# Layer 0's attention: where the softmax sums of a batch are turned into divisors

## The chip, the cores and the metric

The kernel runs on one core of a Trainium2 chip. The metric is the device time of one execution in microseconds (us). Before the change it was 2256.95 us, the median of three runs (2251.18 to 2261.61). A core has engines with queues of their own: TensorE (PE; its weight loads are shown as PEld), VectorE (DVE), ScalarE (ACT), GpSimd (POOL), and SyncE (SP), which here only sends DMAs. Each engine takes its instructions in the order in which they were laid down and waits at an instruction until what it needs is there.

## The reference, cut to what matters

The reference is a four-layer decoder on x of 4 batches, 512 tokens and 128 channels; each layer adds an attention, a cross-attention and a feed-forward part of experts to x. The change touches layer 0's attention alone: 16 heads of 8 channels, causal, with a bias that falls with distance.

```python
att = jnp.einsum('bqhd,bkhd->bhqk', q, k) * scale
att = att / temperature
bias = slopes[:, None, None] * rel[None, :, :]
bias = jnp.where(causal[None, :, :], bias, -jnp.inf)
w = jax.nn.softmax(att + bias[None], axis=-1)
y = jnp.einsum('bhqk,bkhd->bqhd', w, v).reshape(Bc, Tc, Cc)
return y @ W_proj + b_proj
```

So for each batch, query and head there is a sum of exponentials by which 8 channels of y are divided before the projection. x receives the projected y.

## The kernel before, in words

`l0_attn` goes over 16 items, each a batch b and a group g of four heads, in rounds. In round r four items are in work at once: the scores and maxima of item r (`score_units`, eleven units of one or more heads), the exponentials of item r-1 (`exp_units`, ten units; the first five early, at the end of the round, the others late, in the next), the values of item r-2 (`values`), and, where item r-3 closes a batch, the division and the projection of that batch. A round has steps i = 0 to 10. Round 6 is that of batch 0's division, round 10 that of batch 1, round 14 that of batch 2.

The steps in a round that matter here:

- `shift` (i = 0) splits the negated maxima of the item before into three bf16 parts on VectorE; `shift_rows` (i = 2) transposes them on TensorE (L1165), copies them on ACT (`d_rows`, L1167) and puts them into the stacked queries `qs` with four DMAs (L1169). The exponentials of that item read them, first the early ones.
- `load` (i = 7) fetches the stacked parts of queries and keys of item r+2 with six DMAs (L1125, L1126).
- `project`, in the second round of a batch, makes queries and keys of the next batch, splits them into bf16 parts `q3` and `k5`, and sends these to DRAM with four DMAs (`q_parts`, `k_parts`, L1109 and L1111).
- `values` multiplies exponentials by values. The value tile has 32 columns a head, of which 8 are channels and the ninth is one, so the ninth row of a head in the result is its sum of exponentials. ACT copies the result into `ys[b]` (L1207): 128 partitions (four heads of 32 rows), four groups, 512 tokens.
- `sums` (i = 9, in the round in which the last group's values are made) brings the sums into rows of tokens: 16 products of y with a selecting matrix give 128 x 4 x 16; VectorE inverts them (L1219) and splits them into three bf16 parts (`in_three`, from L1290).
- `divide` (i = 1 of the next round) transposes these parts (`turned3`, L1301), copies them on ACT (L1303), spreads each group's inverses over the heads' rows with a product by `pick`, and multiplies y by that, four times 128x512 (L436 is the helper of all such operations, L425 that of all dense products).
- `close` (i = 4 of that round) projects y with 16 products and adds the result to x.

Beside the rounds another chain is woven in at a fixed rate of steps: the norms of the other batches, the small products of the context, then layer 0's cross-attention of batches 0 and 1 and the router of the first two batches (`route`, whose small steps on VectorE end in `w_halves` on POOL, eight transposes on TensorE at L665 and `w_turned`). The order written in the program is not the final one: a planner with its own costs lays the instructions of each engine in an order, in which an instruction may pass others of its engine that are not ready by its reckoning.

Of the kernel before, what the change touches and what calls it, by code (L numbers as in the profile page):

```python
# [13 lines left out]
F32 = mybir.dt.float32  # L14
BF16 = mybir.dt.bfloat16
# [3 lines left out]
ALU = mybir.AluOpType  # L19
# [3 lines left out]
P = 128  # L23
B, S, D = 4, 512, 128
# [267 lines left out]
class Net:  # L292
# [745 lines left out]
    def l0_attn(self, pool, W, Wo):  # L1038
# [3 lines left out]
        nc, tc = self.nc, self.tc  # L1042
# [30 lines left out]
        def biases():  # L1073
            ps = self.mm((1, D))
            self.dot(ps, *[(Wo["bv"][:, g : g + 1], Wo["wp"][:, g * D : g * D + D]) for g in range(4)])
            br = one([1, D], "br")
            self.tt(br, ps, Wo["bp"], ALU.add)
            wp0 = one([P, D], "wp0")
            nc.vector.tensor_copy(wp0, Wo["wp"][:, :D])
            nc.sync.dma_start(wp0[8:9, :], br)  # L1080
            wp.extend([wp0] + [Wo["wp"][:, g * D : g * D + D] for g in range(1, 4)])

        items = [(b, g) for b in range(B) for g in range(4)]
        made, ys, stacks = {}, {}, {}

        def project(b):

            xb = self.tokens(b)
            pq, pk = self.mm(), self.mm()
            self.dot(pq, (W["wq"], xb))  # L1090
            self.dot(pk, (W["wk"], xb))
            q, k = (pool.tile([P, S], F32, tag=n, name=n, bufs=1) for n in "qk")
            nc.vector.tensor_scalar(q, pq, W["bq"], sc, ALU.add, ALU.mult)
            nc.scalar.activation(k, pk, AF.Identity, bias=W["bk"])
            yield
            q3, k5 = pool.tile([P, 3, S], BF16, tag="q3", name="q3"), pool.tile([P, 5, S], BF16, tag="k5", name="k5")
            for a, out in ((q, q3), (k, k5)):
                nc.scalar.copy(out[:, 0], a)
                self.tt(a, a, out[:, 0], ALU.subtract)
            yield  # L1100
            for a, out in ((q, q3), (k, k5)):
                nc.scalar.copy(out[:, 1], a)
                self.tt(out[:, 2], a, out[:, 1], ALU.subtract)
            yield
            nc.gpsimd.tensor_copy(k5[:, 3:5], k5[:, 0:2])
            qd = self.away.tile([16, 24, S], BF16, name=f"q_parts{b}")
            kd = [self.away.tile([16, 24, S], BF16, name=f"k_parts{b}_{c}") for c in range(3)]
            flat = lambda d: d.rearrange("h (d p) t -> (h d) (p t)", p=3)
            nc.sync.dma_start(flat(qd), q3.rearrange("r p t -> r (p t)"))  # L1109
            for c in range(3):  # L1110
                nc.sync.dma_start(flat(kd[c]), k5[:, c : c + 3].rearrange("r p t -> r (p t)"))  # L1111
            stacks[b] = qd, kd
            yield
            ps = self.mm((P, TB, 16, 8))
            for j in range(TB):
                self.dot(ps[:, j].rearrange("p h d -> p (h d)"), (self.tile_of(TB * b + j), W["wv"]))
            nc.scalar.copy(vs[b % 2][:, :, :, :8], ps)
            yield

        def load(b, g):  # L1120

            qd, kd = stacks[b]
            for c in range(3):
                r = slice(24 * c, 24 * c + 24)
                nc.sync.dma_start(qs[g][r], qd[4 * g : 4 * g + 4].rearrange("h r t -> r h t"))  # L1125
                nc.sync.dma_start(ks[g][r], kd[c][4 * g : 4 * g + 4].rearrange("h r t -> r h t"))  # L1126

        def score_units(b, g):

            m = made[b, g, "m"] = pool.tile([P, TB, 4], F32, tag="m", name="m", bufs=2)  # L1130

            def unit(i, h0, per):
                n = (i + 1) * P
                ps = self.mm((P, per, n))
                for h in range(per):
                    nc.tensor.matmul(  # L1136
                        ps[:, h], lhsT=qs[g][:K1, h0 + h, i * P : n], rhs=ks[g][:K1, h0 + h, :n], start=h == 0, stop=False
                    )
                nc.tensor.matmul(  # L1139
                    ps[:, :, i * P :], lhsT=self.identb, rhs=self.causal.unsqueeze(1).to_broadcast([P, per, P]),  # L1140
                    start=False, stop=True,
                )
                nc.vector.tensor_reduce(m[:, i, h0 : h0 + per], ps, AX.X, ALU.max, negate=True)  # L1143

            return [
                lambda i=i, h0=h0, per=per: unit(i, h0, per)
                for i, per in ((3, 1), (2, 1), (1, 2), (0, 4)) for h0 in range(0, 4, per)
            ]

        def shift(b, g):  # L1150

            m = made.pop((b, g, "m"))
            d3 = made[b, g, "d"] = pool.tile([P, TB, 4, 3], BF16, tag="d3", name="d3")
            rest = pool.tile([P, TB, 4], F32, tag="d_rest", name="d_rest")
            nc.vector.tensor_copy(d3[..., 0], m)
            self.tt(rest, m, d3[..., 0], ALU.subtract)
            nc.vector.tensor_copy(d3[..., 1], rest)
            self.tt(d3[..., 2], rest, d3[..., 1], ALU.subtract)
# [49 lines left out]

        inv = {}

        def sums(b):

            y = ys[b]
            ps = self.mm((P, TB, 4, 4))
            for j in range(TB):
                for g in range(4):
                    self.dot(ps[:, j, g], (y[:, g, j * P : j * P + P], W["sums"]))
            den = pool.tile([P, TB, 16], F32, tag="den", name="den")
            nc.vector.reciprocal(den, ps.rearrange("p j g h -> p j (g h)"))  # L1219
            inv[b] = pool.tile([P, TB, 3, 16], BF16, tag="s3", name="s3")  # L1220
            self.in_three(inv[b], den, pool, "s_rest")

        def divide(b):
            y = ys[b]
            dT = self.turned3(inv.pop(b), pool)
            for g in range(4):
                c = self.mm()
                self.dot(c, (pick[:, 4 * g : 4 * g + 4].rearrange("r h i -> r (h i)"), dT))
                self.tt(y[:, g, :], y[:, g, :], c, ALU.mult)

        def close(b):
            y = ys.pop(b)
            ps = self.mm((P, TB, D))
            for j in range(TB):
                self.dot(ps[:, j, :], *[(y[:, g, j * P : j * P + P], wp[g]) for g in range(4)])
            self.add_rows(b, ps)

        def rounds(first, last):
            n = len(items)
            item = lambda i: items[i] if 0 <= i < n else None  # L1240
            if first == 0:
                yield from project(0)
                load(0, 0)
                biases()
                load(0, 1)
                yield
            for r in range(first, last):
                now, prev, old, done = (item(r - i) for i in range(4))
                a = score_units(*now) if now else []
                if prev:  # L1250
                    made["units", prev] = exp_units(*prev)
                late = made.pop(("units", old))[5:] if old else []
                early = made["units", prev][:5] if prev else []
                ahead = project(now[0] + 1) if now and now[1] == 1 and now[0] + 1 < B else iter(())
                for i in range(11):
                    if i == 0 and prev:
                        shift(*prev)
                    if i == 2 and prev:
                        shift_rows(*prev)
                    if i < len(a):  # L1260
                        a[i]()
                    e = late[i : i + 1] if i < 6 else early[i - 6 : i - 5]
                    for unit in e:
                        unit()
                    yield
                    if i == 1 and done and done[1] == 3:
                        divide(done[0])
                        yield
                    if i == 4 and done and done[1] == 3:
                        close(done[0])  # L1270
                        yield
                    if i == 7 and old:
                        values(*old)
                        yield
                    if i == 9 and old and old[1] == 3:
                        sums(old[0])
                        yield
                    if i in (1, 3, 5, 8, 10):
                        next(ahead, None)
                    if i == 7 and item(r + 2):  # L1280
                        load(*item(r + 2))
# [1103 lines left out]
```

## Time and profile before

| what | us |
|---|---|
| median of three runs | 2256.95 |
| the profiled execution | 2272.79 |
| its span, first to last instruction | 2271.0 |
| TensorE busy in the span | 2109.5 (93%) |
| VectorE busy in the span | 1608.1 (71%) |
| layer 0's attention, in the span | about 20 to 280 |
| 16 products of the sums, batch 0 | 94.6 to 98.3 |
| 16 products of the projection, batch 0 | 106.5 to 110.1 |

A busy share is an average over stages with different limits. In the stage of the attention the engines follow one another closely, so the reader should look at the order of instructions in the stretch of a batch's division, at what each waits for, and at the TensorE clock that was granted there: it is a share of full speed, and the products of a stretch with 0.50 take twice their time. Times in the timeline are from the start of the span.

### The profile page before, as it was taken

What the parts mean: (1) busy time and instruction counts of PE and PEld (TensorE: products, weight loads), DVE (VectorE), ACT (ScalarE), POOL (GpSimd) and SP (SyncE); (2) the same over time, 40 slices, a digit from 0 to 9 for tenths busy, and PEclk for the clock granted to TensorE, in tenths of its full rate; (3) what the DMA queues carried; (4) which work ended last, traced back from release to release, by engine and by line L of the source; (5) the groups of instructions that cost most, each with busy time, mean ns of one, the idle gap of its engine ahead of it and who ended that gap; (6) DMA issues with size and microseconds to landing.
All of it is one profiled execution on the core that took longest, in us unless ns stands there. A gap on an engine that the chain in (4) does not pass through costs nothing.

```text
span 2271.0 us, 28138 instructions
## 1 busy us (share of the span) xinstructions
PE 2109.5 (93%) x8946; PEld 1121.5 (49%) x8946; DVE 1608.1 (71%) x4059; ACT 995.4 (44%) x2042; POOL 554.8 (24%) x695
## 2 busy tenths in 40 slices
PE   6999899999999998999999999999999996697778
PEld 3566556544545553444444544444444443564463
DVE  6667576666675769787977797867777765886525
ACT  4556446444325452444434543443343434364421
POOL 1000001000000001433323343333333322336541
PEclk7989999999999999999999999999999998898869
DMA  6321134254453344334334444444443442200022
GB/s 167 99 65 44 45 111 123 62 137 112 112 143 84 105 101 107 75 100 110 110 83 105 114 120 114 124 111 107 114 114 101 111 129 46 94 1 6 20 54 76
DMA packets 88947, 213.26 MB, mean 94 GB/s; under 512 B 21874, under 2 KB 40626, under 8 KB 88542
## 3 DMA queue, kind: packets, MB, share of 16 engines
q1 hardware_dynamic: 85230, 207.52, 34.9%
q0 software_dynamic: 3568, 3.93, 0.6%
q8 instruction: 71, 1.16, 0.2%
q14 instruction: 78, 0.64, 0.1%
HBM read 182.33 MB, written 23.53 MB: 91 GB/s over the span
## 4 chain that ended last, share of the span: by engine, by line
PE 72%; DVE 15%; issue 5%; ACT 3%; POOL 2%; DMA 2%; SPq 1%; another core or an unknown queue 0%; POOLq 0%; DVEq 0%; ACTq 0%
PE mm L425 19%; PE f L425 13%; PE mm L1854 8%; PE s L425 8%; PE acc L1013 6%; PE mm L1826 4%; PE mm L1801 4%; DVE h L436 2%; PE mm L1136 1%; PE mm L1203 1%; PE mm L1181 1%; DVE at_m L1883 1%; DVE m L1143 1%; DVE gvx L436 1%; PE s L515 1%
## 5 line engine op out<-in xcount | busy, mean ns | idle before, releaser
L1762 POOL TENSOR_TENSOR gvx<-gvx 128x512 f32<-128x512 f32 (+1 forms) x256 | 260.3, 1017 | 549.3 <-DVE gvx L436 488.3
L425 PE MATMUL f<-xT,w_l_ffn 128*128 128x512 f32 (+1 forms) x768 | 369.3, 603 | 1.2 <-ACT h L1005 0.7
L1885 ACT ACTIVATE at_e<-mm,at_m 128x512 f32<-128x512 f32 x256 | 173.0, 685 | 293.1 <-DVE at_m L1883 274.3
L425 PE MATMUL mm<-w_l_ffn_qkv,xT 128*128 128x512 f32 x512 | 266.3, 604 | 4.2 <-ACT at_e L1885 1.7
L1854 PE MATMUL mm<-og,w_l_ffn_o 128*128 128x512 f32 x512 | 265.8, 603 | 3.2 <-DVE og L436 3.2
L436 DVE TENSOR_TENSOR h<-h,f 128x512 f32<-128x512 f32 (+1 forms) x192 | 131.1, 684 | 139.9 <-PE f L425 105.3
L1005 ACT ACTIVATE h<-f 128x512 f32<-128x512 f32 x189 | 112.3, 596 | 251.0 <-PE f L425 214.2
L425 PEld LDWEIGHTS f<-xT,w_l_ffn 128*128 128x128 f32 (+1 forms) x768 | 140.2, 192 | 151.0 <-issue 123.6
L1013 PE MATMUL acc<-h,w_l_ffn 128*128 128x512 f32 x378 | 194.8, 600 | 3.5 <-DVE h L436 2.9
L436 DVE TENSOR_TENSOR gvx<-mm,gv 128x512 f32<-128x512 f32 x256 | 174.5, 683 | 20.8 <-PE mm L425 17.1
L436 DVE TENSOR_TENSOR og<-mm,c 128x512 f32<-128x512 f32 x256 | 176.2, 690 | 18.3 <-PE mm L1854 16.0
L1802 ACT COPY eT<-mm 128x512 f32<-128x512 f32 x256 | 137.6, 596 | 83.4 <-PE mm L1801 83.2
L1883 DVE TENSOR_REDUCE at_m<-mm 128x1 f32<-128x512 f32 x256 | 161.1, 681 | 11.7 <-PE mm L425 10.3
L1801 PEld LDWEIGHTS mm<-ident,at_e 128*128 128x128 f32 x1024 | 120.2, 142 | 68.4 <-issue 47.7
L1854 PEld LDWEIGHTS mm<-og,w_l_ffn_o 128*128 128x128 f32 x512 | 91.7, 191 | 114.4 <-issue 90.3
L1801 PE MATMUL mm<-ident,at_e 128*128 128x128 f32 x1024 | 135.1, 274 | 5.3 <-ACT at_e L1885 5.3
L425 PEld LDWEIGHTS mm<-w_l_ffn_qkv,xT 128*128 128x128 f32 x512 | 87.3, 190 | 95.2 <-issue 59.0
L425 PE MATMUL mm<-roped 64*128 64x512 f32 x512 | 131.3, 622 | 1.7 <-DVE roped L436 1.0
L1143 DVE TENSOR_REDUCE m<-mm 128x1 f32<-128x512 f32 (+3 forms) x176 | 104.8, 635 | 32.6 <-PE mm L1139 31.7
L1826 PE MATMUL mm<-eT,v 128*64 128x512 f32 x512 | 118.7, 599 | 0.0
L1013 PEld LDWEIGHTS acc<-h,w_l_ffn 128*128 128x128 f32 x378 | 71.2, 192 | 93.1 <-issue 67.3
L436 DVE TENSOR_TENSOR h<-h,c 128x512 f32<-128x512 f32 x160 | 111.5, 703 | 4.1 <-DMA c<-l_ffn_w 1.3
(453 smaller groups left out, 3529.4 us busy)
## 6 DMA issues: line engine op xcount, KB each, us to landing
c<-gates SPq DMA_DIRECT2D x256, 256.0 KB
c<-l_ffn_w SPq DMA_DIRECT2D x96, 384.0 KB
w_l_ffn<-in_l_ffn SPq DMA_DIRECT2D x26, 576.0 KB
w_l_ffn_qkv<-in_l_ffn_qkv SPq DMA_DIRECT2D x16, 640.0 KB
w_l_ffn_o<-in_l_ffn_o SPq DMA_DIRECT2D x16, 512.0 KB
rot<-qk SPq DMA_DIRECT2D x128, 64.0 KB
d<-inverted SPq DMA_DIRECT2D x64, 128.0 KB
k_parts<-k SPq DMA_DIRECT2D x12, 384.0 KB
```

Source lines behind the costliest of these rows:

```text
L425: self.nc.tensor.matmul(out, lhsT=lhsT, rhs=rhs, start=i == 0, stop=i == len(pairs) - 1)
L436: self.nc.vector.tensor_tensor(out, a, b, op)
L1005: nc.scalar.activation(h, pg, AF.Silu)
L1013: nc.tensor.matmul(acc["t"], lhsT=W["d" + u], rhs=h, start=i == 0, stop=i == n - 1)
L1143: nc.vector.tensor_reduce(m[:, i, h0 : h0 + per], ps, AX.X, ALU.max, negate=True)
L1762: nc.gpsimd.tensor_tensor(x[:, :, :m], x[:, :, :m], x[:, :, m : 2 * m], ALU.add)
L1801: nc.tensor.transpose(p[:, j, :], es[i][hl][:, j * P : j * P + P], self.ident)
L1802: nc.scalar.copy(eT[hl][:, :, i * P : i * P + P], p)
L1826: nc.tensor.matmul(po[64 * hl : 64 * hl + 64, :], lhsT=m["v"][:, j, hl, :], rhs=eT[hl][:, j, :], start=j == 0, stop=j == TB - 1,)
L1854: nc.tensor.matmul(acc, lhsT=W["o"][:, (e - 1) * D : e * D], rhs=hs.pop(e - 1), start=e == 1, stop=e == E)
L1883: nc.vector.tensor_reduce(m, s, AX.X, ALU.max, negate=True)
L1885: nc.scalar.activation(e[:, :n], s, AF.Exp, bias=m, accum_out=den)
```

## The change

For batches 0, 1 and 2 the sums are no longer brought into rows of tokens by TensorE. `sums_away` sends the four rows of y that hold sums (one of each 32) to DRAM with four DMAs, and fetches them back as a tile of 128 partitions by 64, one row per 64 tokens of a head. `inverted`, at i = 1 of the next round, inverts this tile, sends it to DRAM, clears a tile `spread` of 128 x 2048 on POOL and fills nine rows of each head with its inverses by four DMAs that repeat a row. `divide_spread` multiplies y by that tile, two groups at a time, at i = 6 and 7, and `close` comes at i = 9 in place of 4. Batch 3 keeps the old way. The parts of queries and keys now lie in one tile `parts`, and `spread` takes the same place in memory.

```diff
-            q3, k5 = pool.tile([P, 3, S], BF16, tag="q3", name="q3"), pool.tile([P, 5, S], BF16, tag="k5", name="k5")
+            parts = pool.tile([P, 8, S], BF16, tag="parts", name="parts", bufs=1)
+            q3, k5 = parts[:, :3], parts[:, 3:]
...
+        def sums_away(b):
+
+            there = self.away.tile([16, S], F32, name=f"l0_sums{b}")
+            by_row = there.rearrange("(g h) s -> h g s", h=4)
+            for h in range(4):
+                nc.sync.dma_start(by_row[h : h + 1], ys[b][32 * h + 8 : 32 * h + 9])
+            den = pool.tile([P, 64], F32, tag="den", name="den")
+            nc.sync.dma_start(den, there.rearrange("e (k s) -> (e k) s", s=64))
+            inv[b] = den
+
+        def inverted(b):
+            there = self.away.tile([16, S], F32, name=f"l0_inverted{b}")
+            den = inv.pop(b)
+            nc.vector.reciprocal(den, den)
+            nc.sync.dma_start(there.rearrange("e (k s) -> (e k) s", s=64), den)
+
+            spread = spreads[b] = pool.tile([P, 4, S], F32, tag="parts", name="spread", bufs=1)
+            nc.gpsimd.memset(spread, 0.0)
+            by_row = there.rearrange("(g h) s -> h g s", h=4)
+            for h in range(4):
+                nc.sync.dma_start(spread[32 * h : 32 * h + 9], by_row[h].partition_broadcast(9))
+
+        def divide_spread(b, half):
+            y = ys[b][:, 2 * half : 2 * half + 2, :]
+            self.tt(y, y, spreads[b][:, 2 * half : 2 * half + 2, :], ALU.mult)
...
-                    if i == 1 and done and done[1] == 3:
-                        divide(done[0])
-                        yield
-                    if i == 4 and done and done[1] == 3:
-                        close(done[0])
-                        yield
+                    if done and done[1] == 3 and done[0] < B - 1:
+                        if i == 1:
+                            inverted(done[0])
+                        if i in (6, 7):
+                            divide_spread(done[0], i - 6)
+                        if i == 9:
+                            close(done[0])
+                        if i in (1, 6, 7, 9):
+                            yield
+
+                    elif done and done[1] == 3:
+                        if i == 1:
+                            divide(done[0])
+                            yield
+                        if i == 4:
+                            close(done[0])
+                            yield
...
-                        sums(old[0])
+                        (sums_away if old[0] < B - 1 else sums)(old[0])
```

## The prediction

> **What bounds the kernel now.** I read the engine table first, then the stretches around the places that the change touches, then TensorE's and the DMA queue's instructions there in order of time. The span is 2271.0 us of a profiled execution of 2272.79 us; the median of the runs shown is 2256.95 us, 16 us less, so the sum below is made as a difference inside the profiled span and added to the median. A difference of 0.5% is 11.3 us, about what a measurement of this kernel can tell from no change.
>
> ```profile
> span 2271.0 us, 28138 instructions
> PE 2109.5 (93%) x8946; PEld 1121.5 (49%) x8946; DVE 1608.1 (71%) x4059; ACT 995.4 (44%) x2042; POOL 554.8 (24%) x695
> ```
>
> TensorE (PE) is busy 93% of the whole. All of the change lies in layer 0's attention, about 20 to 280 us. Its rounds are in-order on each engine, so what TensorE skips is gained, and whatever it stands waiting for is lost. In the fence below the columns are start, length, engine, line, operation; "idle before" in brackets. The round of batch 0, then of 1 and 2:
>
> ```profile
> 94.56 3.69 PE L425 MATMUL mm<-w_l_attn_qk,y 128*128 128x4 f32 x32
> 103.55 1.02 PE L425 MATMUL mm<-turned,pick 48*128 48x512 bf16 x4 [0.71 <-ACT turned L1303]
> 118.78 0.39 PE L1165 MATMUL mm<-identb,d 128*12 128x128 bf16 x4 [1.61 <-DVE nmr L489]
> 150.89 5.22 PE L425 MATMUL mm<-w_l_attn_qk,y 128*128 128x4 f32 x32
> 163.55 1.86 PE L425 MATMUL mm<-turned,pick 48*128 48x512 bf16 x4 [1.15 <-ACT turned L1303]
> 181.50 0.39 PE L1165 MATMUL mm<-identb,d 128*12 128x128 bf16 x4 [1.41 <-DVE rstd L474]
> 239.37 0.39 PE L1165 MATMUL mm<-identb,d 128*12 128x128 bf16 x4 [1.91 <-DVE d L436]
> ```
>
> The first row of a batch is the sums' 16 products, the second the spreading of the inverses, the third the transposes of the next round's maxima: the mark at which I compare before and after (118.8, 181.5, 239.4 us). The next fence gives the granted clock (before the last two columns):
>
> ```profile
> 117.00:118.00 1.00, 0.18 (x2) 0.00 (x0) 1.00 (x3) 0.70 (x2) 0.00 (x0) 1.00 0.00 0
> 162.00:163.00 1.00, 0.34 (x2) 0.23 (x2) 0.00 (x0) 0.96 (x4) 0.90 (x1) 1.00 0.00 0
> 166.00:167.00 1.00, 1.00 (x5) 0.52 (x4) 1.00 (x3) 0.54 (x1) 0.00 (x0) 0.50 0.00 0
> ```
>
> **What is removed, per batch 0 to 2.** TensorE: the 16 products (3.5 us at full clock, 5.1 in batch 1), four transposes (0.4), four spreading products (1.0 to 1.9), the wait for ACT's copy (0.7 to 1.2). VectorE: the three-part split, about 0.8 us, and four multiplies of 2.48 us. ACT: one copy of 0.57. The sums' products are thin (4 columns), and the clock drops to 0.5 behind them (98.5 to 101.5 us, 153 to 160 us): that loss of 1.6 and 3.5 us goes too.
>
> **What is added.** SP gets ten DMAs a batch: four rows of y out, one load, one store, four loads to nine partitions. VectorE inverts 64 columns (0.56, as now, L1219) and multiplies twice 128x1024; for that the row is 1.22 us, so 2.4 in place of 2.48. POOL clears 128x2048: 3.54 us for two (L1061), 1.8 each; it is idle from 93 to 123 us, so this costs nothing; uncovered it would delay the spreading loads by 1.8. Behind the clearings on POOL stand the bias additions (L550, at 123.0 and 185.8 us now); the third clearing waits for batch 1's multiplies, some ten us before the second of them, so these wait for nothing. The shared buffer costs nothing: its DMAs to DRAM are over at 99.2 us and 156 us (the DMA share falls to nothing there), before the clearing is needed. SP's loads of qs and ks stand behind the store of the inverses, but they serve the round after the next, a round of 12 us away. The close comes five units later, which costs nothing by itself: its 16 products and its addition are the same.
>
> **The chain that takes the sums' place.** Rows for its pieces:
>
> ```profile
> 94.03 2.07 SPq L1111 DMA_DIRECT2D k_parts<-k  x3
> 105.53 2.78 SPq L1169 DMA_DIRECT2D qs<-d_rows  x4
> 927.13 1.31 SPq L1810 DMA_DIRECT2D inverted<-turned  x4
> 930.56 1.12 SPq L1819 DMA_DIRECT2D d<-inverted  x2
> 927.60 1.22 DVE L436 TENSOR_TENSOR rot<-rot,w_const 128x1024 f32<-128x1024 f32 x1
> 1573.73 0.70 DVE L436 TENSOR_TENSOR mm<-mm,d 128x512 f32<-128x512 f32 x1 [2.37 <-DMA d<-inverted]
> ```
>
> A small store is visible to the next DMA 2.1 us after its issue ends (928.44 to 930.56). A load from DRAM has no clean row: from below 1.1 us (d_rows, 1.8 us from its issue's start to the product that needs it, less 0.64 of issue), from above 4.85 (the d of 1573.73 was issued by 1568.9, with 512 KB ahead of it). I take 2.0 for 32 KB and 2.2 for 288 KB, nearer the unloaded row. An issue costs 0.3 to 0.69; I take 0.55. From the end of the inversion: 0.1 + 0.35 + 2.1 (store), 4 x 0.55, 2.2 (landing) = 7.0 us; from below 4.7, from above 10.4.
>
> In the changed order of instructions, SP sends the y rows behind k_parts, then the four d_rows, and only then the load of the sums; VectorE inverts behind the eighth maximum of the round, and the next but two instructions are the two multiplies, with the close's addition and the last maximum behind them; TensorE's close stands behind the fourth early exponential, and everything of the next round behind the close. So the wait holds both engines.
>
> **Batch 0.** From 94.56 TensorE now runs, at rows of full clock: last score unit and exponential 0.67, values' projection 0.9 (1.81 at half clock now), two units 1.0, transposes 0.33, units to the values 1.67 + 1.76, values 2.29, units and exponentials 1.23. That is 104.4; d_rows are sent at 98.6 and hold it 0.6, so 105.0. The last d_rows issue ends at 101.4, the load is issued and lands 0.4 + 2.0 later (103.8), inverted at 104.4; spread landed at 111.4; halves of y at 112.6 and 113.8. The close needs both: 14 of 16 products are left, 3.1 us (16 take 3.57 in 106.50 to 110.07), so 116.9. TensorE stood 7.6 us.
>
> **A rule against the change: the clock.** The row is 162 to 164 us: TensorE 0.34 and 0.45 busy, and the clock is 0.50 up to 169.6 us; at 117 to 119, 1.6 us of idleness drop nothing. The Trainium skill, "TensorE: Matmul & The Clock Gate", Part 1, says that an idle window of some 3.4 us halves the clock and a busy one gives it back. By the rule the wait of 7.6 us costs one window at half speed, 1.7 us; by the row, six us at half speed, 3.0. I take 1.7, since the six us of the row hold a second thin stretch: 118.6. Then the addition, two maxima and the split of the next round, 3.9 us of VectorE: mark at 122.5 against 118.8, +3.7 us.
>
> **Batch 1.** From 150.89: 153.5 by TensorE, but the split ends at 154.3 behind the norm's small steps; ACT does the norm's four rows (1.64), two exponentials (1.0), a copy (0.6) ahead of d_rows: sent from 158.1 to 160.9. Early exponentials wait for them to 160.6, values to 163.3, close reached at 164.5. Load lands 163.3, inverted 163.9, spread 170.9, y 173.3, close 176.4, clock 1.7, mark 182.0 against 181.5: +0.5.
>
> **Batch 2, and the router.** In the changed order the router's block of small steps stands earlier: VectorE does it between the seventh and the eighth maximum, and TensorE has the eight transposes of w_halves before the first early exponential. The block's rows of now sum to 7.2 us (220.4 to 221.0, 225.9 to 228.2, 232.6 to 240.3 without the maxima). Scores of the router end at 217.2, seven maxima at 221.3, router 228.5, POOL 0.3, so TensorE stands from 220.2 to 228.9. Eighth maximum 231.1, inverted 231.7, spread 238.7, y 241.1, close 244.2, 0.9 for the clock (the second wait is shorter), mark 249.0 against 239.4: +9.6. Of the later rounds' waits now (0.91 for w_turned, 0.88, 0.2) 2.0 go: +7.6.
>
> **Sum:** 3.7 + 0.5 + 7.6 = 11.8 us, and nothing behind the rounds gives it back, since TensorE ends them (its last sums at 261.3) and starts the next stage. 2256.95 + 11.8 = 2268.8, say 2269.
>
> **Rivals.** (1) *Waits shorter, no difference seen* (0.33): landings at the lower bounds, 4.7 in place of 7.0 a batch, and no clock drop (1.7 + 1.7 + 0.9): 11.8 - 6.9 - 4.3 = +0.6, 2258. For it: unloaded queues at 105 to 110 us; against it: loads of qs and ks (96 KB each) go between. (2) *Faster* (0.12): y is there when TensorE reaches the close. Then batch 0 has its mark at 112.5 (-6.3), batch 1 at 172.0 (-9.5), batch 2, router wait kept, at +2.2: -13.6, 2243. It decides only where the 7.0 shrinks below nothing, or SP's load passes d_rows; the order speaks against it. (3) *Longer* (0.10): landings at 10.4 and the clock by the row: 11.8 + 10.2 + 3.9 = 2283. (4) That the change does not do what it says is excluded: the products of three batches are not in the new order, only batch 3's.
>
> **How the numbers follow.** Likeliest, as summed, 0.45: 2269, own range 2262 to 2276. The range 2252 to 2284 takes in rivals 1 and 3 and leaves out the faster one. The likeliest lies at the bound of 0.5% (2268.2), so some 0.42 of its chance and 0.10 of rival 3 is slower, rival 1 and the other 0.03 are the same, rival 2 faster.
>
> **What would show it.** In the new profile: TensorE idle some 7 us ahead of the close of batches 0 and 1, ended by VectorE's y; VectorE's y waiting for the DMA of spread; clock 0.5 behind it; TensorE idle some 8 us ahead of the w_halves transposes. Wrong if the y multiplies wait for less than 3 us, if TensorE's idle time falls elsewhere, or if the router's block overlaps.

## The result, and the profile after

The changed kernel takes 2279.45 us (median of four runs, 2278.67 to 2279.67); the kernel before, on the same chip, 2259.28 us (2251.18 to 2264.16). The ratio is 1.0086, 95% interval 1.0060 to 1.0112: slower by some 20 us. The forecast was 2269 us, with a slower kernel as the likeliest sign. The range 2252 to 2284 holds the time; the middle is 10 us too low, of which 2.3 are the kernel before, whose median was 2256.95 when the forecast was made.

The engine table of the profiled execution (2279.67 us):

```profile
span 2277.9 us, 27950 instructions
PE 2095.2 (92%) x8826; PEld 1106.4 (49%) x8826; DVE 1607.3 (71%) x4041; ACT 993.7 (44%) x2039; POOL 558.5 (25%) x698
```

TensorE does 14 us less, and the kernel is longer. Where the time goes is seen in TensorE's instructions in order of time (start, length, line; in brackets the idle time before, and what ended it), the rows that answer to the marks shown of before:

```profile
114.03 0.77 PE L425 MATMUL mm<-wp,y 128*128 128x128 f32 x2 [8.82 <-DVE y L436]
123.02 0.39 PE L1166 MATMUL mm<-identb,d 128*12 128x128 bf16 x4 [1.69 <-DVE d L436]
179.83 0.77 PE L425 MATMUL mm<-wp,y 128*128 128x128 f32 x2 [9.63 <-DVE y L436]
190.00 0.39 PE L1166 MATMUL mm<-identb,d 128*12 128x128 bf16 x4 [1.68 <-DVE d L436]
236.81 1.02 PE L665 MATMUL s<-ident,w_halves 128*16 128x128 f32 x4 [8.51 <-POOL w_halves L658]
250.63 0.56 PE L425 MATMUL mm<-wp,y 128*128 128x128 f32 x2 [4.45 <-DVE y L436]
259.59 0.39 PE L1166 MATMUL mm<-identb,d 128*12 128x128 bf16 x4 [1.69 <-DVE d L436]
304.66 1.02 PE L1013 MATMUL acc<-h,w_l_ffn 128*128 128x512 f32 x2
```

TensorE stands 8.8, 9.6 and 4.5 us ahead of the three closes until VectorE has multiplied y, and in batch 2 another 8.5 us ahead of the router's transposes. The marks lie at 123.0, 190.0 and 259.6 us, where they lay at 118.8, 181.5 and 239.4: later by 4.2, 8.5 and 20.2 us. The last row, the first product that sums experts in the next stage, stood before at:

```profile
281.46 1.08 PE L1013 MATMUL acc<-h,w_l_ffn 128*128 128x512 f32 x2
```

So the attention has cost 23.2 us at its end. The spans differ by 6.9 us only, because the profiled execution of the kernel before, 13.5 us above its median, lost time in the last stage. These are the weight loads of the slots' transposes there (ns: least, median, greatest; first and last start in us), before and after:

```profile
L830 PEld LDWEIGHTS f<-ident,slots x32: 139/230/231, 2161.0 to 2203.5; 128*128 128x128 f32 x32
```

```profile
L830 PEld LDWEIGHTS f<-ident,slots x32: 139/142/231, 2187.6 to 2217.5; 128*128 128x128 f32 x32
```

The median load took 230 ns before and 142 after: in this stretch the clock was at half for 32.3 us before and for 12.3 after. The lag of 26.6 us at the first of these loads is 14.0 at the last; the other 7.1 us are made up behind them and were not taken apart. The change touches nothing there. So the medians of the times, not the two spans, tell its price.

What TensorE waits for is seen in the DMA queue and on VectorE in batch 0 (SPq rows are issues):

```profile
101.59 0.32 SPq L1221 DMA_DIRECT2D den<-l_sums  x1
103.31 0.55 DVE L1227 RECIPROCAL den<-den 128x64 f32<-128x64 f32 x1 [1.57 <-DMA den<-l_sums]
103.89 0.34 SPq L1228 DMA_DIRECT2D l_inverted<-den  x1
105.42 1.36 SPq L1234 DMA_DIRECT2D spread<-l_inverted  x4
112.66 2.36 DVE L436 TENSOR_TENSOR y<-y,spread 128x1024 f32<-128x1024 f32 x2 [7.00 <-DMA qs<-q_parts]
```

The last row names a load of queries as releaser; the multiply reads nothing of it. It is the spread tile that came in then (in the run below without the loads of queries and keys, the releaser named is the spread tile). From the end of the last spreading issue (106.78) to the multiply are 5.9 us: I call that the landing. In batches 1 and 2 it is 5.7 and 4.7 us.

And the granted clock, the number before the last two, in stretches of 4 us (the first number behind the comma is the time in which TensorE was busy):

```profile
108.00:112.00 4.00, 0.00 (x0) 0.00 (x0) 0.00 (x0) 0.00 (x0) 0.00 (x0) 0.50 0.67 76
116.00:120.00 4.00, 4.00 (x31) 3.87 (x31) 0.24 (x1) 0.00 (x0) 0.00 (x0) 0.78 0.02 4
180.00:184.00 4.00, 4.00 (x19) 3.88 (x20) 0.82 (x1) 0.00 (x0) 1.80 (x1) 0.50 0.00 0
```

Behind each wait the close runs in part at half clock. From its first product to the addition that reads it are 5.7, 6.9 and 5.7 us, where 3.8 are enough (see the second experiment); so 1.9, 3.1 and 1.9 us are lost.

### The profile page after: what moved, and what is told of

Its sections match the earlier page's. It is cut to its first block, busy times and chain, and to the rows that moved or that the text cites. A ratio compares the mean times of both kernels' runs of the same rounds, so it can differ in the third digit from the quotient of the medians.

```text
span 2277.9 us, 27950 instructions
## 1 busy us (share of the span) xinstructions
PE 2095.2 (92%) x8826; PEld 1106.4 (49%) x8826; DVE 1607.3 (71%) x4041; ACT 993.7 (44%) x2039; POOL 558.5 (25%) x698
## 5 line engine op out<-in xcount | busy, mean ns | idle before, releaser
L1923 DVE TENSOR_REDUCE at_m<-mm 128x1 f32<-128x512 f32 x256 | 161.2, 683 | 11.5 <-PE mm L425 10.4
L1190 ACT ACTIVATE e<-mm 128x512 f32<-128x512 f32 (+1 forms) x176 | 92.5, 559 | 57.5 <-PE mm L1186 53.7
## 6 DMA issues: line engine op xcount, KB each, us to landing
d<-inverted SPq DMA_DIRECT2D x64, 128.0 KB
```

The lines of the kernel that those rows point to most:

```text
L1923: nc.vector.tensor_reduce(m, s, AX.X, ALU.max, negate=True)
```

## The experiments

The theory tested (T): TensorE stands in order for the inverses' way through DRAM, above all for the landing of the spread tile, runs at half clock behind that, and in batch 2 also stands for the router, which the planner lays earlier. The rivals: the added traffic itself costs (R), or the later place of the close and the order around it (Q). The kernels of the first four runs share the runs of the kernel before (2259.68 us); the other seven ran on two chips where that kernel takes 2280 to 2281 us, so ratios are compared. The changed kernel was not run on those two; the three kernels closest to it (rows in another order, six loads left out, router later) have 1.0072 to 1.0087 there. The loads of L830 shown above have a median of 230 ns in every trace from those two chips and of 142 ns in the four from the first, so a part of the 20 us between the chips lies in the last stage. Each trace is one execution.

**Batch 2 left as it was.**

```diff
-                    if done and done[1] == 3 and done[0] < B - 1:
+                    if done and done[1] == 3 and done[0] < 2:
...
-                        (sums_away if old[0] < B - 1 else sums)(old[0])
+                        (sums_away if old[0] < 2 else sums)(old[0])
```

> Batches 0 and 1 keep the new way, batch 2 is divided as before the change. Theory T (TensorE stands in order ahead of each close for the inverses' way through DRAM, runs at half clock behind that, and in batch 2 stands also ahead of the router's transposes, which the planner lays earlier): batch 2 alone costs 12.9 us in the traces (marks of rounds 13 to 16: 45.2 us before, 58.2 after), so the time is about 13 us below the changed kernel, 2266 beside 2279, still some 8 above the kernel before; the transposes of w_halves stand again in pieces behind the last maxima and TensorE waits less than 2 us ahead of them. Rival R (the cost is the traffic of the added DMAs and clearings, in equal parts for each batch): a third of 20 us is saved, 2272.

Measured: 2272.44 us, ratio 1.0063 (1.0036 to 1.0090). The time is R's number (2272); T's 2266 would be a ratio of 1.0028, outside the interval. The trace, though, shows what T says: the waits ahead of the closes of batches 0 and 1 are there, and the router's is gone.

```profile
113.12 0.77 PE L425 MATMUL mm<-wp,y 128*128 128x128 f32 x2 [8.70 <-DVE y L436]
178.07 0.77 PE L425 MATMUL mm<-wp,y 128*128 128x128 f32 x2 [9.29 <-DVE y L436]
293.32 1.08 PE L1013 MATMUL acc<-h,w_l_ffn 128*128 128x512 f32 x2
```

The end of the attention (last row) is 11.3 us earlier than in the changed kernel: in these two executions batch 2 is about half of the loss at this point. The 12.9 us were expected between the marks of rounds 13 and 16, and there only 6.9 are gone (51.3 us in place of 58.2); 1.9 lie ahead of that stretch and 2.6 behind it. In the stretch the clock is at half for 17 us (221.6 to 238.6), from 2.5 us behind the start of the old sums of batch 2 (219.1) on, where the kernel before, with its sums at 212.3, had 6.9 us of it (221.0 to 227.9): 5 us lost.

**The spreading loads left out** (tile filled with ones, so y is not divided; the rest unchanged).

```diff
-            nc.gpsimd.memset(spread, 0.0)
+            nc.gpsimd.memset(spread, 1.0)
...
-            for h in range(4):
-                nc.sync.dma_start(spread[32 * h : 32 * h + 9], by_row[h].partition_broadcast(9))
```

> The four loads that spread the inverses are left out in all three batches and the tile is filled with ones, so y is not divided; sums, inversion, its store, the clearing, both multiplies and the order of the close remain. T: the waits ahead of the close (8.8, 9.6 and 4.5 us) fall to about 1, 1 and 0 us and the half clock behind the first two goes (2.4 us each): some 25 us below the changed kernel, 2254, a little below the kernel before (2259); the router's wait of 8.5 us in batch 2 stays. Rival Q (it is the later place of the close and the router's order that cost, whatever y waits for): less than 10 us are saved, 2270 or more.

Measured: 2252.08 us, ratio 0.9967 (0.9954 to 0.9981), as T had it. The closes of all three batches start without an idle time; the router's wait stays; the clock through the first close is full:

```profile
106.84 0.44 PE L425 MATMUL mm<-wp,y 128*128 128x128 f32 x2
216.48 1.02 PE L665 MATMUL s<-ident,w_halves 128*16 128x128 f32 x4 [8.44 <-POOL w_halves L658]
276.08 1.02 PE L1013 MATMUL acc<-h,w_l_ffn 128*128 128x512 f32 x2
```

TensorE's order of the products and the place of the close are those of the changed kernel, and 28.6 us at the attention's end are gone: Q falls as the main cause. The run takes away more than the landing. With nothing to wait for, VectorE multiplies y at 103.2 us in batch 0, ahead of the inversion, so the whole way through DRAM is off the path; and the traffic of the loads is gone too, so this run does not tell T from R (the run with the close at step 7 does). All that costs some 27 us (1.0086 against 0.9967); the rest of the change gains 7.5. Batch 2 splits likewise: from the mark of round 13 to that of round 15 were 34.6 us before, 46.2 after, and are 41.7 here. So with the spreading wait away, the new order with the router's block still costs 7.1 us there; the wait costs the other 4.5.

**The close one round later.** If the wait is the cost, a close that comes when the tile is there should gain. First with the multiplies at steps 0 and 1 and the close at step 3 of the round after:

```diff
+                    if last and last[1] == 3 and last[0] < B - 1:
+                        if i in (0, 1):
+                            divide_spread(last[0], i)
+                        if i == 3:
+                            close(last[0])
+                            yield
...
-        net.weave(rounds(7, 11), net.l0_xattn(0, w1, s1), 2.5)
+        net.weave(rounds(7, 11), net.l0_xattn(0, w1, s1), 2.5, 8)
```

(the same for the chain behind it; `last` is item r-4.)

> All three batches the new way, but both multiplies and the close come in the round after (steps 0, 1 and 3), one round of some 12 us later; the chain of the cross-attention and router begins eight steps later, since it reads what the close writes. T: the spread tile has landed when VectorE and TensorE get there, so neither waits; the gain of the removed products shows: the mark of round 7 comes near 112 us (118.8 before), that of round 11 about 16 us earlier than before; the router's transposes still stand ahead of a round's exponentials and cost some of it. In all 2246 (2240 to 2254) beside 2259 before and 2279 after. Rival R (the traffic of the DMAs disturbs loads of the queries and keys, or other engines, wherever the close stands): no better than before, 2262 or more.

Measured: 2269.89 us, ratio 1.0061 (1.0038 to 1.0083): far from the 2246 expected. With batch 2 left as before (bounds 2 in place of B - 1):

> As the kernel with the close a round later, but batch 2 is divided as before the change. T: gain of batches 0 and 1 of 6 and 9 us and the router where it was: 2244 (2238 to 2252). If batch 2 the new way gains as much as batches 0 and 1 once it does not wait, this is 3 to 6 us above the kernel with all three late; if the router's place costs more than the removed products bring, it is below it. Rival R: 2262 or more.

Measured: 2262.28 us, ratio 1.0010 (0.9994 to 1.0027). By the times alone, R had both right (2262 or more). The step of mine that failed in both: I took the close to come a round of 12 us later, but from steps 6 and 7 of one round to steps 0 and 1 of the next are only five steps. VectorE came to the multiplies of batch 0 at 111.4 us, where it had come at 105.7.

```profile
109.28 0.39 PE L1166 MATMUL mm<-identb,d 128*12 128x128 bf16 x4 [1.35 <-DVE d L436]
113.67 2.36 DVE L436 TENSOR_TENSOR y<-y,spread 128x1024 f32<-128x1024 f32 x2 [2.30 <-DMA qs<-q_parts]
115.04 0.76 PE L425 MATMUL mm<-wp,y 128*128 128x128 f32 x2 [4.16 <-DVE y L436]
```

The mark is 9.5 us earlier than before, better than expected, but the tile still lands at 113.7 us: VectorE waits 2.3 and TensorE 4.2 us, with half clock again (112.0 to 118.8 us). In the kernel with batch 2 left as before, TensorE waits 6.2 us there.

**Four steps later still.** Multiplies at steps 4 and 5, close at step 7:

```diff
-                        if i in (0, 1):
-                            divide_spread(last[0], i)
-                        if i == 3:
+                        if i in (4, 5):
+                            divide_spread(last[0], i - 4)
+                        if i == 7:
```

> All three batches the new way, multiplies at steps 4 and 5 and the close at step 7 of the round after. In the kernel with steps 0, 1 and 3 the spread tile landed at 113.7 us while VectorE stood for it from 111.4 and TensorE from 110.9 to 115.0; some 4 us later in the order it should be there. T: no wait for y ahead of the close in batches 0 and 1 and none of more than 1 us in batch 2, no half clock behind it; 8 us less than the kernel with the close at step 3, 2262 (2254 to 2266); the router's wait of 8.6 us ahead of the w_halves transposes remains and is what keeps it from beating the kernel before. Rival R (it is not the wait; the chains woven in later, or the DMAs, cost): within 3 us of that kernel, 2267 or more.

Measured: 2280.79 us, ratio 0.9994 (0.9979 to 1.0008): by ratio 2258 where the first group's chip has 2260, a gain of 15 us over the close at step 3 where 8 were expected. No wait for y ahead of the first two closes, and a new one in its place:

```profile
116.29 0.61 PE L1182 MATMUL mm<-qs,ks 99*128 99x512 bf16 x1 [4.49 <-DMA qs<-d_rows]
231.31 1.02 PE L665 MATMUL s<-ident,w_halves 128*16 128x128 f32 x4 [8.63 <-POOL w_halves L658]
247.96 0.46 PE L425 MATMUL mm<-wp,y 128*128 128x128 f32 x2 [0.96 <-DVE y L436]
```

From the kernel with the close at step 3 only these steps differ; the DMAs are all there, the wait for y is not, and the time falls by 15 us: this is what tells T from R. But the exponentials now wait 4.5 us for the shift rows, 3 KB each, whose issues stand right behind the spreading loads in the queue. In this execution, at 2289.05 us the longest of the twelve, the spreading loads went out 2 us later than in most (see the last section); in the first run of the next kernel, where they did not, the same wait is 1.8 us. So a part of R may be true after all: the traffic can cost where the close no longer hides it. That it is the spreading loads which hold up the rows is read from the order in the queue and was not tested. With batch 2 left as before the change:

> As the one before, but batch 2 is divided as before the change. T: no wait ahead of either close and no router ahead of its round: what the removed products of two batches bring is left over, some 8 to 10 us: 2250 (2244 to 2256) beside 2259 before. Rival R: 2259 or more, as with the close at step 3 (2262).

Measured: 2274.98 us beside 2280.12, ratio 0.9973 (0.9958 to 0.9987). Again on another chip:

> The kernel with batches 0 and 1 the new way, closed at step 7 of the round after, and batch 2 as before the change, once more on another chip: 0.9973 was measured of the kernel before. T: again below 1, 0.996 to 0.999. If that was chance: 1.000 or above.

Measured: 2274.59 us beside 2280.99, ratio 0.9974 (0.9963 to 0.9985). This version beats both kernels, if by little: it is 0.26% below the kernel before, with the interval below 1 both times, and by ratios some 1.1% below the changed one. In the first of the two runs:

```profile
113.41 0.39 PE L1182 MATMUL mm<-qs,ks 99*128 99x512 bf16 x1 [1.82 <-DMA qs<-d_rows]
114.41 0.77 PE L425 MATMUL mm<-wp,y 128*128 128x128 f32 x2
171.92 0.46 PE L425 MATMUL mm<-wp,y 128*128 128x128 f32 x2 [0.43 <-DVE y L436]
276.85 1.08 PE L1013 MATMUL acc<-h,w_l_ffn 128*128 128x512 f32 x2
```

The closes hardly wait, and the attention ends 4.6 us before that of the kernel before. In the second run it is 2.4 us, with 4.4 us of waiting for shift rows ahead of the first close.

**What sets the landing: pieces, bytes, or the neighbours.** Three runs with TensorE's order of the changed kernel. Rows in DRAM ordered so that a row to be repeated is one piece of 8 KB, not four of 2 KB:

```diff
-            by_row = there.rearrange("(g h) s -> h g s", h=4)
+            by_row = there.rearrange("(h g) s -> h g s", h=4)
```

> As the changed kernel, but the rows in DRAM are ordered head within group first, so that the row that a spreading load repeats is one piece of 8 KB in place of four of 2 KB (a quarter of the descriptors). Same bytes, same order of instructions. If the landing of 5.9, 5.7 and 4.7 us from the last issue is set by the number of pieces, the landing falls to some 3 us, TensorE's waits ahead of the close from 8.8, 9.6 and 4.5 to about 6, 7 and 2, and the time by some 8 us to 2271. If it is set by the bytes[...], or by the loads of queries and keys beside them, nothing moves: 2279.

Measured: ratio 1.0072 (1.0047 to 1.0098); landings 5.8, 5.8 and 4.6 us. The number of pieces is not it.

A quarter of the bytes:

```diff
-                nc.sync.dma_start(spread[32 * h : 32 * h + 9], by_row[h].partition_broadcast(9))
+                nc.sync.dma_start(spread[32 * h : 32 * h + 9, :1], by_row[h][:1].partition_broadcast(9))
```

> As the changed kernel, but the four spreading loads carry the rows of the first of four groups only (72 KB in place of 288); the rest of the tile is filled with ones, so three of four groups of y are not divided. Same number of DMAs, same order of instructions. If bytes set the landing, it falls from 5.9, 5.7 and 4.7 us behind the last issue to some 3 us, TensorE's waits ahead of the close from 8.8, 9.6 and 4.5 to about 6, 7 and 3, and the time lies some 8 to 12 us below the changed kernel, +0.4% against the kernel before. If it is the fixed price of a load from DRAM behind a store (or the loads of queries and keys in front), the landing stays above 5 us and the time where the changed kernel's is, +0.8%.

Measured: ratio 1.0031 (1.0017 to 1.0046), as the byte theory had it. In batch 0:

```profile
106.75 1.36 SPq L1234 DMA_DIRECT2D spread<-l_inverted  x4
109.52 1.22 DVE L436 TENSOR_TENSOR y<-y,spread 128x1024 f32<-128x1024 f32 x1 [2.51 <-DMA spread<-l_inverted]
110.89 0.77 PE L425 MATMUL mm<-wp,y 128*128 128x128 f32 x2 [4.34 <-DVE y L436]
```

The landings are 1.4 and 1.5 us in batches 0 and 1. TensorE waits 4.3 and 5.3 there, 4.5 and 4.4 less than in the changed kernel, and the landings are 4.5 and 4.2 shorter: the wait follows the landing nearly one to one. One thing else differs: the multiply of the other two groups reads nothing that is loaded and runs at 102.7 us, ahead of the inversion, so a single multiply stands behind the landing.

The neighbours' loads left out in rounds 6 and 10:

```diff
-                    if i == 7 and item(r + 2):
+                    if i == 7 and item(r + 2) and not (done and done[1] == 3 and done[0] < B - 1):
```

> As the changed kernel, but the six loads of queries and keys that stand around the spreading loads in rounds 6 and 10 are left out (the scores of those two items are made from older rows, so the result is another). If the 576 KB of these loads hold up the spread tile, the landing in batches 0 and 1 falls from 5.9 and 5.7 us to the 4.7 of batch 2, which has no such loads beside it, the two multiplies' wait by as much and a little more through the free queue ahead of the spreading loads, and the time by some 3 to 4 us, +0.7% against the kernel before. If the spread alone sets its landing, nothing moves, +0.86%.

Measured: ratio 1.0087 (1.0063 to 1.0110); landings 4.45, 4.4 and 4.5 us.

```profile
105.78 1.37 SPq L1234 DMA_DIRECT2D spread<-l_inverted  x4
111.60 2.36 DVE L436 TENSOR_TENSOR y<-y,spread 128x1024 f32<-128x1024 f32 x2 [5.64 <-DMA spread<-l_inverted]
```

The loads of queries and keys hold the tile up by some 1.4 us in batches 0 and 1, and TensorE's waits there fall to 7.5 and 8.5 us. That is too little for the time to show, and no gain was measured. So of a landing of 5.9 us three quarters of the bytes are worth 4.5, with the neighbours still there, and the neighbours 1.4, with all the bytes still there. The two were not left out together, and other numbers of receiving partitions were not tried.

**The router's chain begun 20 steps later**, so that its transposes stand directly ahead of batch 2's close:

```diff
-... net.route("l0_ffn", first, w1, s1)), 2.5)
+... net.route("l0_ffn", first, w1, s1)), 2.5, 20)
```

> As the changed kernel, but the chain with the router begins 20 steps later, which puts the eight transposes of w_halves directly ahead of batch 2's close, where TensorE waits anyway. T: the wait of 8.5 us ahead of the early exponentials goes and overlaps with the wait for y: 7 us less, 2272. Rival: the wait only moves (VectorE does the router's block ahead of the eighth maximum and so later the inversion), or the chain's end hangs behind the rounds and delays the next stage: 2278 or more.

Measured: ratio 1.0076 (1.0053 to 1.0099), no different from the changed kernel's. The wait moved, as the rival had it:

```profile
233.44 1.63 PE L515 MATMUL s<-ident,xn 128*128 128x128 f32 x4 [5.01 <-ACT xn L491]
248.72 1.02 PE L665 MATMUL s<-ident,w_halves 128*16 128x128 f32 x4 [1.51 <-POOL w_halves L658]
256.03 0.77 PE L425 MATMUL mm<-wp,y 128*128 128x128 f32 x2 [4.50 <-DVE y L436]
```

TensorE now stands for a norm of the same chain (5.0 us), less for the router, and as long as ever for y; batch 2's close begins 5.4 us later than in the changed kernel. Whether another lead would free batch 2 was not tried.

## Why the prediction was right, point by point

- **"TensorE idle some 7 us ahead of the close of batches 0 and 1":** 8.8 and 9.6. TensorE came to batch 0's close at 105.2 us (forecast 105.0), and the inversion ended at 103.9 (104.4).
- **The chain of 7.0 us** from the inversion to the multiplies was 8.8, 9.0 and 7.6: inside its bounds of 4.7 to 10.4, but by the wrong terms. In batch 0 the store was visible 1.2 us after its issue, not 2.1; four issues took 1.36 us, not 2.2; the landing was 5.9, 5.7 and 4.7 us, not 2.2. That last one is the mis-sized term. I took the unloaded row of 3 KB pieces for 288 KB that go to nine partitions, and the loaded bound of 4.85 was not an upper one. That the sum came out only 0.6 to 2.0 us short is in part luck: a landing 2.5 to 3.7 us too short was set against a store and issues 1.4 to 1.8 us too long.
- **The clock: 1.7 us by the rule, 3.0 by the row.** The forecast was 1.7, 1.7 and 0.9; measured were 1.9, 3.1 and 1.9. (The row's stretch at half clock is 6.8 us, 163.0 to 169.8, not six.) Neither price is right for every wait, and the traces say why (the rows below have the columns of the clock's rows above). In each of the thirteen, all changes of the clock lie whole intervals of 3.41 us apart: in the changed kernel it drops at 107.50, 124.57, 172.36, 230.38, 250.87, 261.11 and 285.00 us, steps of 5, 14, 17, 6, 3 and 7 intervals. Batch 0's close began at 114.03, just ahead of an interval in which TensorE was busy throughout (114.33 to 117.74), and got the full clock at its end. Batch 1's began at 179.83, when the interval from 179.18 on had already begun; at its end the clock stayed at half, until the next one was over (186.01).

```profile
179.18:182.60 3.42, 2.77 (x13) 2.68 (x14) 1.64 (x2) 0.00 (x0) 1.67 (x1) 0.50 0.00 0
182.60:186.01 3.41, 3.41 (x18) 3.41 (x18) 0.00 (x0) 0.00 (x0) 0.13 (x1) 0.50 0.00 0
```

- **The term that was missing** is the rounds behind. From the mark of round 7 to that of round 8 the clock fell again (0.50 from 124.6 to 128.0 us, behind the idle time of 1.7 us at 121.3 to 123.0), and 1.8 us went. I had reasoned that 1.6 us of idleness drop nothing, from one execution in which that happened to be so (see the last section).
- **Batch 0, +3.7:** the mark is 4.2 later. **Batch 1, +0.5:** from the mark of round 9 (143.2 before, 149.3 after) to that of round 11 it is 2.4 more, by the longer landing and the longer half clock.
- **Batch 2, +9.6 at its mark:** 11.5 from round 13 to 15. The mechanism of two waits stood: 8.5 us for the router (forecast 8.7), then 4.5 for y. **"Of the later rounds' waits 2.0 go":** this failed. From that mark to the first product of the next stage the changed kernel takes 3.0 us more, not 2.0 less; the clock is at half for 3.4 us around 263, where it was full before, and for 13.6 us from 285 on, behind the old sums of batch 3, where before it was 10.2; half of these 6.8 us more is 3.4 lost.
- **The sum:** 11.8 against 23.2 at the end of the attention and 20 in the medians. Rival 3 (2283), which priced landing and clock at their upper ends, came nearer than the likeliest case: 3.6 us off the measured time in place of 10.4. Rival 2, y there in time, did not come; made by leaving the loads out, it gains 7.5 us, not the 13.6 it was priced at.

## What to carry to other kernels

A product that an in-order engine does itself can be cheaper than a way through memory that no work hides: price the chain to its last landing, with its bytes and its neighbours in the queue, and only then count the products that go. If it is longer than what stands between, move the reader, not by a number of steps but to where the trace says that the data are there, and look again for the next reader in the same queue. Whatever is saved or waited also shifts where the clock's intervals fall on the work that follows, and these differ from one execution to the next: a sum of instructions holds to some microseconds here and no better.

## What was not expected of the hardware

- A broadcast of 288 KB to 4 x 9 partitions landed 4.45 us after its last issue with no loads of queries and keys beside it and 5.9 with them; 72 KB landed after 1.4 with them. Pieces of 8 KB in place of 2 KB changed nothing (5.8).
- The way from the store of the inverses to the next issue took 1.2 us in most executions, but in batch 0 of two it took 3.2 and 3.4 us: the kernel with the close at step 7 and all three batches, and the second run of the one with two batches. The first run of that same kernel had 1.2. Where it took long the exponentials waited 4.4 to 4.5 us in place of 1.8. Why was not found out.
- The same idle time of 1.7 us behind the close cost a half clock in some executions and not in others: from the mark of round 7 to that of round 8 it is 13.95 us in the changed kernel and with the spreading loads out, 12.35 to 12.37 with batch 2 left as before, with other rows in DRAM and with a quarter of the bytes. What differs is where the intervals of 3.41 us fall. In the changed kernel one interval holds all of the idle time; with batch 2 left as before the border lies in the middle of it:

```profile
121.16:124.57 3.41, 1.72 (x16) 1.08 (x15) 3.28 (x16) 1.75 (x4) 0.00 (x0) 1.00 0.00 0
124.57:127.98 3.41, 3.41 (x19) 2.07 (x17) 2.34 (x7) 1.81 (x4) 0.00 (x0) 0.50 0.02 6
119.15:122.57 3.42, 2.38 (x21) 1.58 (x19) 2.62 (x7) 1.42 (x3) 0.00 (x0) 1.00 0.00 0
122.57:125.98 3.41, 2.77 (x26) 2.00 (x27) 3.28 (x16) 2.14 (x4) 0.00 (x0) 1.00 0.00 1
```

  So it is in all eight traces with the close in its own round. In the three where the clock fell (the changed kernel, the loads out, the router later) TensorE was busy for 1.72 to 1.78 us of that interval; in the five where it did not, the least is 1.97 (the kernel before). The rule that the forecast used asks for an idle interval; here one that was half busy was enough. It is no sharp border everywhere: in the first run of the kernel with the close at step 7 and two batches, an interval with TensorE busy for 1.74 us (from 240.4 on) kept the full clock.
- The clock also fell where TensorE counts as busy: with batch 2 left alone it is at half from within its old sums, thin products of 4 columns, for 17 us, where in the kernel before the same sums ran at full clock. Here too the intervals differ: the one that ends at 221.6 holds two thirds of these products, while before a border at 214.2 halves them. That this is the reason fits, but was not tested. The row of that stretch in the kernel that leaves batch 2 alone (TensorE busy 16.33 of 17 us, clock 0.52):

```profile
221.00:238.00 17.00, 16.33 (x78) 11.95 (x79) 9.25 (x28) 7.27 (x12) 0.34 (x1) 0.52 0.00 1
```
